# Layer 3 of a four-layer convolution/sequence kernel: transfers moved to the front of each time step, the logarithm moved ahead of the next exponentials, and the matmuls that open a sum put in separate places

## The chip, the cores and the metric

The kernel runs on one core of a Trainium2 chip. Five engines work from queues of their own, each strictly in the order written: TensorE (PE, with its weight loads shown as PEld), VectorE (DVE), ScalarE (ACT), GpSimd (POOL) and SyncE (SP), which in this part of the kernel only issues DMAs. An instruction that must wait holds everything behind it in its own queue. The metric is the device time of one execution in microseconds (us).

## The reference, cut to what matters

Four layers run one after another over `x` of shape (2, 128, 64, 64). Only the last one, layer 3, is touched. Each pixel's 128 channels are read as a sequence of 8 tokens of 16 channels, and a small state-space model runs along the tokens:

```
xi, z = split(seq @ in_proj_w.T)
xs    = silu(causal_conv(xi))                       # 32 channels
dt, Bm, Cm = split(xs @ x_proj_w.T, [1, 17])
dt    = softplus(dt @ dt_proj_w.T + dt_proj_b)
dA    = exp(dt[..., None] * A)                      # 32 channels x 16 states
dBx   = dt[..., None] * Bm[:, :, None, :] * xs[..., None]
h     = dA_t * h + dBx_t                            # token after token
y     = sum over states of h * C_t
out   = ((y + xs * D) * silu(z)) @ out_proj_w.T
```

The result goes through a group norm and a SiLU and is added to the layer's input.

## The kernel before, in words

Layer 3 works on 16 chunks (2 images x 8 chunks of 512 pixels). A chunk keeps its 512 pixels along the free dimension. Its 8 tokens are taken in 4 time steps, k = 0 to 3, of two neighbouring tokens each (o = 0 and 1; at k = 0 the first token needs no recursion). State is held as tiles of 128 partitions (4 states of a group x 32 channels) by 4 groups by 512 pixels, and the work on a tile is cut into two halves of 128x1024.

The order of the work is written out by hand: one loop over steps `s`, and in every step four places g = 0 to 3 (plus a tail, place 4). A place is named (k, g) here. At each place the loop issues fixed work, then what two tables hold: `first` (issued early in the place) and `extra` (issued at its end). `manual_schedule` keeps that order on every engine; waits come only from data and from buffers.

The fixed work of a step, for its own chunk:

- `mul` (POOL, L1278): A x h of the token before, 128x1024. `add` (L1283): D = D + that product, most on DVE, one half a step on POOL. `advance()` hands these out: it issues products until it has issued one DVE addition.
- `db_` (DVE, L1265): D of the **next** step times `dt x` taken from the PSUM tile `rx`; `rx_` (PE, L1261) spreads `dt x` of one token over the partitions. `rx` has two buffers.
- `da_` (ACT, L1271): four exponentials A = exp(dt x A) of the **next** step, read from `dtr`.
- `pc_` (PE, L1295, tile `q`) and `hc_` (DVE, L1300): product of A h with C, for the step **before**; `y_` (PE, L1313) adds it up in PSUM tile `y`, which has one buffer. The sums for the third unit and after come later, `y_(k, 3)` two steps on.

In `first` and `extra` stands the work that prepares later chunks, and what ends a chunk. `fut2` is the chunk two ahead, `fut` the next:

- `xs_`, `sz_` (PE into `misc`, SiLU on ACT) of `fut2`, in step 2. PSUM tile `misc` has one buffer, so each waits for the eviction before it.
- `dt_` (PE, then Abs and Relu on ACT), `e_exp` (ACT, L1211), `e_ln` (ACT, L1214): softplus. `dt_add` (POOL, L1217) finishes dt, `dtx_` (POOL, L1220) makes `e` = dt x xs, and `put` (SP, L1224) writes dt to a DRAM tile `ddt`.
- `b_` (PE L1184, copy on ACT L1191, then the DMA `rows<-bs` on SP, L1193), `c_`/`cb_`: B and B x C.
- `cbx_` (PE, into `misc`) and `ecb_` (DVE, L1251): the part of y that needs no recursion. `ecb_` overwrites `dt`, so it also waits until `put` has read it. `cbx_(1)` needs `misc` back from `ecb_(0)`.
- `load` (SP, L1244): `D<-rows`, 4 DMAs of 256 KB for one token of the step two ahead; six `D` buffers. `spread` (SP, L1232): `dtr<-ddt`, 8 DMAs of 64 KB (4 at k = 0) for the step two ahead; two buffers.
- `y0_` (PE, L1305): opens the sum y with D x xs and with `ecb_`'s result; `yg_` (DVE, L1318) gates y when it is done; `xr_`, `bn_` end the chunk.

On SP every DMA is bound to one of eight completion counters in turn, so one that is issued waits for the landing of the eighth before it.

Of the kernel before, what the change touches and what calls it, by code (L numbers as in the profile page):

```python
# [57 lines left out]
def conv_seq_kernel(ctx: ExitStack, tc: tile.TileContext, a: dict, out: bass.AP):  # L58
    nc = tc.nc
    mm = nc.tensor.matmul  # L60
# [4 lines left out]
    def gt(shape, name, pool=None, **kw):  # L65
        return (pool or gp).tile(shape, F32, tag=name, name=name, **kw)
# [14 lines left out]
    ident = cst[:, _CI : _CI + 128]  # L81
# [17 lines left out]
    with ExitStack() as c0:  # L99
# [36 lines left out]
        diag_d = gt([P, 2, P], "diag_d", wp)  # L136
# [347 lines left out]
        nk = len(chunks)  # L484
# [12 lines left out]
        with tc.manual_schedule():  # L497
            c, c1 = chunks[:2]
# [113 lines left out]
            for k, c in enumerate(chunks):  # L612
# [3 lines left out]
                def at(u):  # L616
                    return (c, u) if 0 <= u < 16 else ((old, u + 16) if u < 0 else (new, u - 16))
# [115 lines left out]
    with ExitStack() as c1:  # L733
# [272 lines left out]
        for n, j in enumerate(jobs):  # L1006
# [10 lines left out]
            if jobs[n - 1].layer == 1:  # L1017
                for ci in range(NCH):
                    c = Conv(jobs[n - 1].b, ci)
# [70 lines left out]
    with ExitStack() as c3:  # L1090
# [50 lines left out]
        diag_d = gt([P, P], "diag_d3", wp)  # L1141
# [10 lines left out]
        class Chunk3:  # L1152
# [148 lines left out]

            def y0_(self, i):
                self.y = ps.tile([P, T], F32, tag="y", name="y")
                for w, rhs in ((diag_d, self.xs), (ident, self.dt)):
                    mm(self.y, lhsT=w, rhs=rhs[:, i, :], start=w is diag_d, stop=False,  # L1305
                       skip_group_check=True)

            def y_(self, k, u):
                i, j = PLACE[k]
# [93 lines left out]
        with tc.manual_schedule():  # L1403
            c, c1 = chunks[:2]
            for i in range(2):
                c.xs_(i)
            for i in range(2):
                c.sz_(i)
            c.b_()
            for i in range(2):  # L1410
                c.dt_(i)
            c.e_exp()
            c.e_ln()
            c.dt_add()
            c.put()
            c.dtx_()
            c.spread(0)
            c.load(0, 0)
            c.load(0, 1)
            c.c_()  # L1420
            c.cb_()
            for i in range(2):
                c.cbx_(i)
                c.ecb_(i)
            for i in range(2):
                c1.xs_(i)
            c1.sz_(0)
            norms = [Norm(b) for b in range(B)]
            c.rx_(0, 0)
            for s in range(-1, len(steps) + 3):  # L1430
                (pc_, pk), (cc, ck), (nc_, nk) = at(s - 1), at(s), at(s + 1)
                (n2, n2k) = at(s + 2)
                ci, k = divmod(s, 4)
                fut = chunks[ci + 1] if s >= 0 and ci + 1 < len(chunks) else None
                fut2 = chunks[ci + 2] if ci + 2 < len(chunks) else None
                old = chunks[ci - 1] if ci > 0 else None
                nrm = norms[0] if ci in (NCH, NCH + 1) else None


                if cc is None:  # L1440
                    todo = []
                elif ck == 0:
                    todo = [("m", 1, 0), ("m", 1, 1), ("v", 1, 0), ("g", 1, 1)]
                elif ck == 3:
                    todo = [("m", 0, 0), ("m", 0, 1), ("v", 0, 0), ("g", 0, 1), ("m", 1, 0), ("m", 1, 1)]
                else:
                    todo = [("m", 0, 0), ("m", 0, 1), ("v", 0, 0), ("v", 0, 1), ("m", 1, 0),
                            ("m", 1, 1), ("v", 1, 0), ("g", 1, 1)]

                def advance():  # L1450

                    while todo:
                        w, o, hf = todo.pop(0)
                        if w == "m":
                            cc.mul(ck, o, hf)
                        else:
                            cc.add(ck, o, hf, V if w == "v" else G)
                        if w == "v":
                            return

                first, extra = {}, {}

                def more(key, *what, at=extra):
                    at.setdefault(key, []).extend(what)

                if cc is not None:
                    more((1, 2), lambda: cc.y0_(0), at=first)
                    more((3, 2), lambda: cc.y0_(1), at=first)  # L1470
                    more((3, 0), lambda: cc.yg_(0))
                if old is not None:
                    more((1, 0), lambda: old.yg_(1))
                    more((1, 2), old.xr_)
                    more((2, 0), old.bn_)
                if fut2 is not None and s >= 0:
                    more((2, 1), lambda: fut2.xs_(0))
                    more((2, 2), lambda: fut2.xs_(1))
                    more((2, 3), lambda: fut2.sz_(0))
                if fut2 is not None:  # L1480
                    more((3, 0), lambda: fut2.sz_(1), at=first)
                    more((3, 1), fut2.b_)
                    more((3, 2), lambda: fut2.dt_(0))
                    more((3, 3), lambda: fut2.dt_(1), fut2.e_exp)
                if fut is not None:
                    more((0, 0), fut.e_ln)
                    more((0, 1), fut.c_)
                    more((0, 2), fut.cb_, fut.dt_add, fut.dtx_)
                    more((0, 3), fut.put)
                    more((0, 3), lambda: fut.cbx_(0))  # L1490
                    more((1, 0), lambda: fut.ecb_(0), lambda: fut.cbx_(1))
                    more((1, 1), lambda: fut.ecb_(1))
                if 0 <= ci < B:
                    more((1, 3), lambda: nc.sync.dma_start(kept[ci], x[:, ci, :]))
                if n2 is not None:
                    more((k, 1), lambda: n2.load(n2k, 0))
                    more((k, 2), lambda: n2.load(n2k, 1))
                    more((k, 3), lambda: n2.spread(n2k))
                    more((k, 2), lambda: n2.rx_(n2k, 0), at=first)
                if nc_ is not None:  # L1500
                    more((k, 0), lambda: nc_.rx_(nk, 1), at=first)
                if ci == NCH:
                    more((2, 2), nrm.first)
                    more((2, 3), nrm.second)
                    more((2, 4), nrm.third)
                    more((3, 1), nrm.fourth)
                if ci == NCH + 1:
                    more((2, 3), *[lambda j=j: nrm.silu(j) for j in range(4)])
                    more((0, 0), lambda: nrm.load(0), lambda: nrm.load(1))
                    more((2, 4), lambda: nrm.store(0, G), lambda: nrm.load(2))  # L1510
                    more((3, 2), lambda: nrm.store(1, V), lambda: nrm.load(3))
                    more((3, 4), lambda: nrm.store(2, G), lambda: nrm.store(3, V))

                (older, ok) = at(s - 2)
                units = 0 if pc_ is None else 2 if pk == 0 else 4

                sums = {}
                for u in range(units):
                    g = (2 + u) if pk == 0 else max(2, u + 1) if pk == 2 else u + 1
                    sums.setdefault(g, []).append(u)  # L1520
                for g in range(4):
                    if g < units:
                        prepare()
                    if g == 0 and older is not None and ok:
                        older.y_(ok, 3)
                    for f_ in first.get((k, g), []):
                        f_()
                    for u in sums.get(g, []):
                        pc_.y_(pk, u)
                    if g < units:  # L1530
                        pc_.hc_(pk, g)
                    if nc_ is not None and nk != 3:
                        nc_.db_(nk, g // 2, g % 2)
                    elif nc_ is not None and g % 2 == 0:
                        nc_.db_(nk, 0, g // 2)
                    if g == 0 and nc_ is not None:
                        nc_.da_(nk)
                    if g < 3:
                        advance()
                    for f_ in extra.get((k, g), []):  # L1540
                        f_()
                while todo:
                    advance()
                for f_ in extra.get((k, 4), []):
                    f_()
                if s < 0:
                    prepare()
            n1 = norms[1]
            n1.load_all()
            n1.first()  # L1550
            n1.second()
            n1.third()
            n1.fourth()
            for j in range(4):
                n1.silu(j)
                n1.store(j, V)
# [111 lines left out]
```

## Time and profile before

| | us |
|---|---|
| median of the runs shown (3 runs, 6790.3 to 6802.03) | 6790.45 |
| the profiled execution | 6801.13 |
| its span, first to last instruction | 6799.3 |
| layer 3 in it, from about | 5629 to the end |
| busy in 5700 to 6660: PE / DVE / POOL / ACT, of 960 us | 793.8 / 755.7 / 695.9 / 408.0 |
| mean granted TensorE clock there | 0.86 |

The busy rows are read within the stage, since the four layers have different limits. A granted clock of 0.86 is a mean of full and half speed. Layer 3 is very regular: the instruction `dt_add` of the 15 chunks that are prepared inside the loop starts at 5703.17 for the first and 6663.00 for the last, so one chunk takes (6663.00 - 5703.17) / 14 = 68.56 us. Lines that begin with a time are instructions, with start, duration, engine, line, tiles; a bracket at the end is the engine's idle time before it and what ended that.

### The profile page before, as it was taken

The numbers are of one execution on the slowest core, as the hardware profiler recorded it, in microseconds if no ns is written. First come the engines' busy times: TensorE is split into PE (matmuls) and PEld (weight loads), VectorE is DVE, ScalarE is ACT, GpSimd is POOL, SyncE is SP. The second block draws the span as 40 slices with busy tenths as digits, with TensorE's granted clock in tenths as the row PEclk, the third lists the DMA queues.
The fourth block names the chain that finished last, engine by engine and source line by source line (L and its number), as shares of the span: only waits on it lengthen the run. The fifth ranks groups of instructions, "written<-read, shape, count | busy, mean of one in ns | idle before, by whom it ended". The sixth has DMA issues, their size and how long they took to land. (4 is left out here: it accounts for less than half of the span.)

```text
span 6799.3 us, 66250 instructions
## 1 busy us (share of the span) xinstructions
PE 5964.9 (88%) x19980; PEld 2797.7 (41%) x19980; DVE 5548.7 (82%) x4456; ACT 4472.3 (66%) x7737; POOL 5378.7 (79%) x2471
## 2 busy tenths in 40 slices
PE   8888888888888888888889999999999996888887
PEld 2222222222222222222248877887788881222221
DVE  7999999999999999999977665665566764877877
ACT  7887788877788777887765654554555553444442
POOL 6999999999999999999966665555566664777776
PEclk8888777877887778877789999999999996888987
DMA  6556655655666566665610000000000005665664
GB/s 183 144 148 162 164 148 143 150 145 144 157 152 153 145 150 154 155 149 144 155 47 1 5 3 1 1 1 1 1 1 1 1 1 128 150 157 137 171 148 124
DMA packets 397882, 700.60 MB, mean 103 GB/s; under 512 B 73801, under 2 KB 76242, under 8 KB 396882
## 3 DMA queue, kind: packets, MB, share of 16 engines
q1 hardware_dynamic: 396640, 694.32, 41.4%
q8 instruction: 157, 2.57, 0.2%
q14 instruction: 203, 1.66, 0.1%
q10 hardware_dynamic: 882, 2.04, 0.1%
HBM read 584.80 MB, written 111.28 MB: 102 GB/s over the span
## 5 line engine op out<-in xcount | busy, mean ns | idle before, releaser
L384 POOL TENSOR_TENSOR dbu<-dus,bs 128x1024 f32<-128x1024 f32 x1024 | 2447.1, 2439 | 117.4 <-DVE h L428 103.6
L428 DVE TENSOR_TENSOR_SCAN h<-da,hst,dbu 128x1024 f32<-128x1024 f32 x896 | 2092.6, 2342 | 86.8 <-ACT dbu L412 80.2
L397 ACT ACTIVATE da<-dts,aneg 128x512 f32<-128x512 f32 (+1 forms) x2048 | 1410.1, 689 | 356.3 <-DVE h L428 319.3
L924 POOL TENSOR_TENSOR sum<-sum,sc 128x1024 f32<-128x1024 f32 x384 | 906.7, 2361 | 491.7 <-ACT sc L919 487.9
L886 ACT COPY sc<-s 128x512 f32<-128x512 f32 x1024 | 597.6, 585 | 859.5 <-PE s L881 745.8
L881 PE MATMUL s<-q,k 128*128 128x256 f32 x4096 | 1052.0, 380 | 7.1 <-DVE k L858 3.5
L893 DVE TENSOR_TENSOR mx<-mx,s 128x512 f32<-128x512 f32 x896 | 610.0, 681 | 546.0 <-ACT sc L886 544.8
L451 PE MATMUL y<-hc,cst 128*32 128x512 f32 x4096 | 884.2, 758 | 193.2 <-DVE hc L440 180.1
L936 PE MATMUL av<-sc,v 128*128 128x256 f32 x4096 | 1049.5, 379 | 2.5 <-ACT sc L919 2.5
L440 DVE TENSOR_TENSOR hc<-h,pc 128x1024 f32<-128x1024 f32 x704 | 843.6, 1198 | 10.1 <-PE y L451 8.3
L881 PEld LDWEIGHTS s<-q,k 128*128 128x128 f32 x4096 | 776.6, 190 | 141.0 <-issue 29.0
L936 PEld LDWEIGHTS av<-sc,v 128*128 128x128 f32 x4096 | 768.8, 190 | 103.2 <-ACT sc L919 3.9
L438 POOL TENSOR_TENSOR hc<-h,cs 128x1024 f32<-128x1024 f32 x320 | 770.6, 2408 | 1.2 <-issue 1.2
L417 PE MATMUL pc<-xd,sel 16*128 16x512 f32 x1024 | 709.0, 783 | 1.5 <-DVE hc L440 1.3
L1278 POOL TENSOR_TENSOR A<-A,D 128x1024 f32<-128x1024 f32 x224 | 523.9, 2358 | 129.9 <-DVE D L1283 101.1
L916 DVE TENSOR_TENSOR sc<-sc,pm 128x1024 f32<-128x1024 f32 x512 | 620.9, 1214 | 0.9 <-PE pm L912 0.9
L919 ACT ACTIVATE sc<-sc 128x1024 f32<-128x1024 f32 x512 | 541.9, 1059 | 8.7 <-DVE sc L916 8.1
L341 PE MATMUL misc<-xd,w_dt 9*128 9x512 f32 x504 | 365.7, 812 | 127.8 <-ACT x L480 69.1
L451 PEld LDWEIGHTS y<-hc,cst 128*32 128x32 f32 x4096 | 126.3, 120 | 847.5 <-DVE hc L440 416.6
L1283 DVE TENSOR_TENSOR D<-D,A 128x1024 f32<-128x1024 f32 x128 | 282.6, 2208 | 130.9 <-POOL A L1278 130.9
L412 ACT ACTIVATE dbu<-hst,dbu,df 128x1 f32<-128x1 f32 x896 | 337.6, 377 | 62.4 <-POOL dbu L384 39.9
L1295 PE MATMUL q<-xs,lc 32*128 32x512 f32 x896 | 301.8, 687 | 36.0 <-DVE A L1300 35.9
(263 smaller groups left out, 7722.0 us busy)
## 6 DMA issues: line engine op xcount, KB each, us to landing
dts<-ddt SPq DMA_DIRECT2D x512, 256.0 KB, 5.4
dus<-ddu SPq DMA_DIRECT2D x512, 256.0 KB, 5.1
D<-rows SPq DMA_DIRECT2D x448, 256.0 KB, 5.9
bs<-rows SPq DMA_DIRECT2D x1024, 64.0 KB, 4.9
cs<-rows SPq DMA_DIRECT2D x1024, 64.0 KB, 3.3
ddt<-dt SPq DMA_DIRECT2D x128, 256.0 KB, 2.0
ddu<-dtu SPq DMA_DIRECT2D x128, 256.0 KB, 4.1
dtr<-ddt SPq DMA_DIRECT2D x448, 64.0 KB, 4.7
```

Of the source, the lines that this page charges most:

```text
L384: nc.gpsimd.tensor_mul(t, self.dus[q], _bc(self.bs[g], 1, [P, 2, T]))
L397: act(t[:, i, sl], self.dts[q][:, i, sl], AF.Exp, scale=an[:, g, 2 * q + i : 2 * q + i + 1])
L417: mm(t, lhsT=sel[32:48, 4 * g : 4 * g + 4, :].rearrange("p n d -> p (n d)"), rhs=self.xd[32:48, :], start=True, stop=True)
L428: nc.vector.tensor_tensor_scan(ho, ai, bi, init, ALU.mult, ALU.add)
L438: nc.gpsimd.tensor_mul(t, self.h[u], _bc(self.cs[gq(u)[0]], 1, [P, 2, T]))
L440: nc.vector.tensor_mul(t, self.h[u], _bc(self.pc[u // 2], 1, [P, 2, T]))
L451: mm(self.y[q // 2][r : r + 32, :], lhsT=sum4, rhs=self.hc[u][:, i, :], start=False, stop=(u % 8 >= 6), skip_group_check=True)
L881: mm(p[:, o, :], lhsT=j.k[m // 8][:, m % 8 * P : m % 8 * P + P], rhs=self.q, start=True, stop=True)
L893: nc.vector.tensor_max(self.mx, self.s[0][:, 0:2, :] if u == 1 else self.mx, self.p[u])
L916: nc.vector.tensor_sub(s, s, _bc(self.pm[:, :], 1, [P, 4, NQ]))
L924: nc.gpsimd.tensor_add(self.sum, self.s[0] if w == 1 else self.sum, self.s[w])
L936: mm(self.av, lhsT=self.job.v[m // 8][:, m % 8, :], rhs=self.s[u // 2][:, m % 4, :], start=(m == 0), stop=(m == 31))
```

## The change

Nothing is computed otherwise; instructions move to other places of the loop.

- SP: `spread`, then `load(.., 0)` of the step two ahead go to place 0, `load(.., 1)` to place 1 (before: `load` at 1 and 2, `spread` at 3).
- ACT: `e_ln` goes from (0, 0) of the next step to right behind `e_exp`, at (3, 2). `dt_` goes from (3, 2) and (3, 3) to (3, 1) and (3, 2); `b_` from (3, 1) to (3, 3), so behind the logarithm.
- POOL: `dt_add` and `dtx_` from (0, 2) to (0, 0), ahead of the POOL addition of step 0. `c_` and `cb_` go to (0, 0) and (0, 1).
- PE: both `rx_` of the step two ahead stand together at the end of place 3 (before: one at place 2, the other at place 0 of the following step). `xs_` and `sz_` go to places 0 to 3 of step 2. `y0_` is split: `y0_(0)` at (1, 1) and `y1_(0)` at (1, 3), both for i = 1 at (3, 1) (before: both at (1, 2) and both at (3, 2)).
- DVE: in place 3 `hc_` comes behind `db_`.
- Ahead of the loop: `sz_` of chunk 1 and both `rx_` of the first step.

```diff
             def y0_(self, i):
                 self.y = ps.tile([P, T], F32, tag="y", name="y")
-                for w, rhs in ((diag_d, self.xs), (ident, self.dt)):
-                    mm(self.y, lhsT=w, rhs=rhs[:, i, :], start=w is diag_d, stop=False,
-                       skip_group_check=True)
+                mm(self.y, lhsT=diag_d, rhs=self.xs[:, i, :], start=True, stop=False,
+                   skip_group_check=True)
+
+            def y1_(self, i):
+                mm(self.y, lhsT=ident, rhs=self.dt[:, i, :], start=False, stop=False,
+                   skip_group_check=True)
...
-            c1.sz_(0)
+            for i in range(2):
+                c1.sz_(i)
             norms = [Norm(b) for b in range(B)]
-            c.rx_(0, 0)
+            for o in range(2):
+                c.rx_(0, o)
...
                 if cc is not None:
-                    more((1, 2), lambda: cc.y0_(0), at=first)
-                    more((3, 2), lambda: cc.y0_(1), at=first)
+                    more((1, 1), lambda: cc.y0_(0), at=first)
+                    more((1, 3), lambda: cc.y1_(0), at=first)
+                    more((3, 1), lambda: cc.y0_(1), lambda: cc.y1_(1), at=first)
...
                 if fut2 is not None and s >= 0:
-                    more((2, 1), lambda: fut2.xs_(0))
-                    more((2, 2), lambda: fut2.xs_(1))
-                    more((2, 3), lambda: fut2.sz_(0))
+                    more((2, 0), lambda: fut2.xs_(0))
+                    more((2, 1), lambda: fut2.xs_(1))
+                    more((2, 2), lambda: fut2.sz_(0))
+                    more((2, 3), lambda: fut2.sz_(1))
                 if fut2 is not None:
-                    more((3, 0), lambda: fut2.sz_(1), at=first)
-                    more((3, 1), fut2.b_)
-                    more((3, 2), lambda: fut2.dt_(0))
-                    more((3, 3), lambda: fut2.dt_(1), fut2.e_exp)
+                    more((3, 1), lambda: fut2.dt_(0))
+                    more((3, 2), lambda: fut2.dt_(1), fut2.e_exp, fut2.e_ln)
+                    more((3, 3), fut2.b_)
                 if fut is not None:
-                    more((0, 0), fut.e_ln)
-                    more((0, 1), fut.c_)
-                    more((0, 2), fut.cb_, fut.dt_add, fut.dtx_)
+                    more((0, 0), fut.c_, fut.dt_add, fut.dtx_)
+                    more((0, 1), fut.cb_)
+                    more((0, 2), lambda: fut.cbx_(0))
                     more((0, 3), fut.put)
-                    more((0, 3), lambda: fut.cbx_(0))
                     more((1, 0), lambda: fut.ecb_(0), lambda: fut.cbx_(1))
                     more((1, 1), lambda: fut.ecb_(1))
...
                 if n2 is not None:
-                    more((k, 1), lambda: n2.load(n2k, 0))
-                    more((k, 2), lambda: n2.load(n2k, 1))
-                    more((k, 3), lambda: n2.spread(n2k))
-                    more((k, 2), lambda: n2.rx_(n2k, 0), at=first)
-                if nc_ is not None:
-                    more((k, 0), lambda: nc_.rx_(nk, 1), at=first)
+                    more((k, 0), lambda: n2.spread(n2k), lambda: n2.load(n2k, 0))
+                    more((k, 1), lambda: n2.load(n2k, 1))
+                    more((k, 3), lambda: n2.rx_(n2k, 0), lambda: n2.rx_(n2k, 1))
...
-                    if g < units:
+                    if g < min(units, 3):
                         pc_.hc_(pk, g)
...
+                    if g == 3 and units == 4:
+                        pc_.hc_(pk, g)
```

## The prediction

> **What bounds the kernel now.** I read the page's 40 slices first: layer 3 holds the last sixth of the span, and no engine there is full. Then the waits by engine, in 5760 to 6660 (engine and line, what it waited for: us in total, times, longest):
>
> ```profile
> POOL dt L1217 <- ACT e L1214: 146.8, 13, 12.6
> ...
> DVE D L1283 <- POOL A L1278: 109.1, 38, 7.5
> ...
> PE misc L1165 <- DVE dt L1251: 120.9, 13, 10.9
> ...
> ACT L1271 <- DMA dtr<-ddt: 115.7, 13, 10.3
> ```
>
> Once a chunk POOL stands about 11 us at `dt_add`, PE about 9 us at `cbx_(1)`, ACT 9 us at `da_`. The timeline of one chunk shows that it is one stall, handed on. ACT, POOL, SP, DVE, PE:
>
> ```profile
> 6512.19 1.06 ACT L1211 ACTIVATE e<-e 128x1024 f32<-128x1024 f32 x1
> 6518.37 4.27 ACT L1271 ACTIVATE A<-dtr,aneg 128x1024 f32<-128x1024 f32 x4 [5.13 <-DMA dtr<-ddt]
> ...
> 6523.95 1.06 ACT L1214 ACTIVATE e<-e 128x1024 f32<-128x1024 f32 x1
> ```
>
> ```profile
> 6501.23 9.32 POOL L1278 TENSOR_TENSOR A<-A,D 128x1024 f32<-128x1024 f32 x4
> 6510.62 2.36 POOL L1283 TENSOR_TENSOR D<-D,A 128x1024 f32<-128x1024 f32 x1
> 6525.09 2.34 POOL L1217 TENSOR_TENSOR dt<-dt,e 128x1024 f32<-128x1024 f32 x1 [12.10 <-ACT e L1214]
> 6527.50 2.34 POOL L1220 TENSOR_TENSOR e<-dt,xs 128x1024 f32<-128x1024 f32 x1
> 6529.80 4.64 POOL L1278 TENSOR_TENSOR A<-A,D 128x1024 f32<-128x1024 f32 x2
> ```
>
> ```profile
> 6502.62 0.34 SPq L1193 DMA_DIRECT2D rows<-bs  x1
> 6503.07 3.85 SPq L1244 DMA_DIRECT2D D<-rows  x8
> 6507.36 8.78 SPq L1232 DMA_DIRECT2D dtr<-ddt  x8
> 6516.25 3.68 SPq L1244 DMA_DIRECT2D D<-rows  x8
> 6527.45 0.34 SPq L1224 DMA_DIRECT2D ddt<-dt  x1
> ```
>
> ```profile
> 6532.18 3.35 DVE L1283 TENSOR_TENSOR D<-D,A 128x1024 f32<-128x1024 f32 x1 [7.53 <-POOL A L1278]
> ...
> 6536.04 0.67 DVE L1251 TENSOR_TENSOR dt<-e,misc 128x512 f32<-128x512 f32 x1
> ```
>
> ```profile
> 6525.26 1.12 PE L1261 MATMUL rx<-e,cst 32*128 32x512 f32 x2
> 6536.77 2.07 PE L1165 MATMUL misc<-cb,nsum 128*128 128x512 f32 x2 [10.39 <-DVE dt L1251]
> ...
> 6546.49 3.24 PE L1313 MATMUL y<-A,cst 128*32 128x512 f32 x4
> 6549.66 1.98 PE L1323 MATMUL misc<-sz,lo 128*128 128x512 f32 x4
> ```
>
> Read it in this order. SP's loads wait behind `rows<-bs`, so `dtr` of step 1 lands late and `da_` starts at 6518.37, 5.13 us late. The logarithm stands behind `da_` on ACT and ends at 6525.0. `dt_add` needs it, and POOL's products of step 1 stand behind `dt_add`: POOL is idle 12.10 us. DVE's addition waits 7.53 us for the product; `ecb_(0)` stands behind that addition; PE waits 10.39 us for `ecb_(0)`. After that gap PE runs at half speed: two-row groups take 2.07 us where the same groups took 1.12, until 6549.66, so for 12.8 us.
>
> **The clock I use.** t = 0 is POOL's first product of step 3, at 6493.30; the next chunk's is at 6562.65, t = 69.35. Before: `dt_add` starts at t = 31.8, `da_(1)` ends at 29.3, the product of step 1 starts at 36.5, DVE's addition ends at 42.2, `ecb_(0)` starts at 42.7.
>
> **The change part by part, for one chunk.**
>
> *Logarithm and `dt_`.* `yg_` before `y0_(1)` ends at 6499.63 (t = 6.3) and frees `y`. From there PE issues `y0_`, `y1_`, `dt_(0)`, one `pc_`, two `y_`, `dt_(1)`: seven groups of 1.05 us (the pitch in the rows at full clock), to t = 13.7. ACT then takes Abs and Relu (0.69 + 0.68), exp 1.06, table load 1.28, logarithm 1.06: t = 18.4 instead of 31.7. The number of table loads stays four a chunk (SiLU, exp, ln, exp), so that costs nothing. POOL is free at t = 17.25, so its wait falls from 12.1 to about 1 us.
>
> *POOL.* `dt_add` and `dtx_` 2.34 each, then the POOL addition that is now behind them 2.36, then the product: t = 25.4 to 27.8, against 36.5 to 38.9. `da_(1)` follows `b_`'s copy (0.57) and a table load (1.28): it runs t = 20.2 to 24.5, hence in time; its `dtr` is issued in step 3 ahead of `rows`. DVE gets to the addition when its own work of step 0 ends, at 6524.6 (t = 31.3) as now; it ends at about t = 33.
>
> *SP: the new wait.* `rows<-bs` now waits for a copy that stands behind the logarithm: t = 18.9 instead of 9.3. Behind it on SP stand 8 `dtr`, 8 `D`, and then `put`. Before, `put` was alone. What does that cost? In the timeline rows + 8 D + 8 dtr, 2816 KB, took from 6502.62 to the landing at 6518.1, 15.5 us. Rows + dtr + D + `put` are 3328 KB; at the same pace 18.3 us, so `put` lands at t = 37.2. The lower bound is 16 issues (4.01 + 3.68 us) and `put`'s median landing of 2.8: t = 30. I take 37.2, since DMAs of one burst share the engines. `ecb_(0)` must wait for it: start 37.2 instead of 42.7. The gain of 11 us on POOL is cut to 5.5 here.
>
> *PE and its clock.* From `y0_(1)` to its `cbx_(1)` PE took 6501.97 to 6526.38, 24.4 us, and gets `b_` in addition (1.05): it is free at t = 31.8 and waits 6.1 us for `ecb_(0)` at 37.9. Gaps in this layer of 2.17 us and less were followed by full-speed groups, those of 3.35 and more by half speed. So the clock still falls. I take the same 12.8 us at half speed.
>
> *`rx_` moved back.* In step 1 the `rx` of step 3 stood behind `cbx_`, `pc_`, `y0_`, `y1_`; it now stands behind `xr_` and two unpaired `y_` too. At half speed that is 12.8 us for `cbx_`, `pc_`, `y0_`, `y_` (3.24) and `xr_`, then at full speed `y1_` 1.0, `y_` 1.9, `rx` 1.05: ready at 37.9 + 16.8 = 54.7, used by `db_` to 55.8; the addition of step 2 behind it ends at 57.0, against 58.3 now. So 1.3 us of the gain are left here. Then it grows again: `bn_`, `hc_`, addition (0.69 + 1.13 + 1.2) end at 60.0, where they now end at 63.7, since `bn_` and `q` are no longer late; product 2.37 and POOL addition 3.22 end the step at 65.6. With the shortest half-speed stretch seen (5780.9 to 5788.3, 7.4 us) the same sum gives 62.8, against 66.4 for that chunk before.
>
> *The rest.* `xs_`/`sz_` one place earlier, `hc_` behind `db_` in place 3, `c_`/`cb_` earlier: no new work. `xs_(1)` waits for ACT behind `da_` as now (0.36 us), up to 2 us, covered by `q` having two buffers; the `c_` group ends at about t = 21, DVE reaches `cb_` at 20.4, under 1 us. Both are in DVE's margin before its addition; if PE were late by more, each would move the chunk one for one. The two groups ahead of the loop cost at most 2 us once.
>
> **Sum.** 69.4 - 65.6 and 66.4 - 62.8: 3.7 us a chunk, call it 4.0, since a gap of 6.1 instead of 10.4 should leave the shorter stretches more often. Fifteen chunks have the stall: 60 us. The profiled execution's 6801.13 becomes 6741; it lies 10.7 above the median of the runs, so the prediction is 6730.
>
> The Trainium skill says in "TensorE: Matmul & The Clock Gate", What's actually happening, that full clock comes back after about 3.4 us of sustained work. The row differs: 12.8 us of uninterrupted half-speed groups. By the rule the lag would be 1.7 us rather than 6.4, and by an estimate from that page the time would be some 40 us lower; no number here uses it.
>
> **Rivals.**
>
> *A. The clock never falls* (0.24). If `put` lands by t = 34.4, `ecb_(0)` ends by 35.1 and the gap is below 3.35 us. For it: 2.8 us median landing. Against: 2 MB are in flight ahead. Then `ecb_(0)` ends at 34.1, `rx` is ready at 45, the POOL/DVE chain runs through: 57.5 us a chunk, 11 less than the mean of 68.56, 165 us: 6625.
>
> *B. Slower: the clock falls at the other gap* (0.18). `y0_(1)` at (3, 1) waits for `yg_`. Where the rows stand now PE would idle 1.0 us there, but if PE comes out of step 2 early, up to 3.3. From 3.35 on the clock falls there, and everything up to `b_` runs at half speed: 3.7 to 6.4 us later (half of 7.4 and 12.8). `rows`, `put` and `ecb_(0)` come as much later, and 65.6 becomes 69.3 to 72. At the middle, 70.7, that is 1.35 us a chunk over now, 20 us: 6811. It decides from a delay of about 4 us on.
>
> The clock gate page of the Trainium skill, HAM oscillation, names idle gaps over about 3.4 us as what brings the clock down; the 3.35 us gap in the trace agrees, and that is the rule that speaks against this change.
>
> *C. Nothing gained* (0.08). `put` lands 4 us later than I take it (41 us), because `dtr`'s small packets slow the burst; then chunk time stays within 1 us: 6775 to 6800.
>
> **Numbers.** The forecast has 0.50, within 6690 to 6765 by its own bounds (2 to 6.7 us a chunk). A and the forecast are faster, 0.74; C and the edge of B are within 0.2% (about 14 us, what a measurement of this kernel can tell from no change), 0.08; the rest of B is slower, 0.18. The range 6628 to 6808 leaves out the lower part of A and the upper of B.
>
> **What would show it.** Right: POOL's idle at `dt_add` at 0 to 3 us, the logarithm directly behind the exponential, `ecb_(0)` waiting for `ddt<-dt`, PE's gap at `cbx_(1)` of 4 to 8 us with 2.08 us groups behind it, `db_` of step 3 waiting for `rx`. Wrong: a PE gap over 3.35 us ahead of `y0_` (B), a granted clock near 1.0 throughout (A), or ACT waiting for `dtr` in a new place.

## The result and the profile after

The changed kernel takes 6770.94 us (median; 6755.09 to 6785.65), the kernel before 6795.49 us beside it (6787.81 to 6802.03). The ratio is 0.9964, interval 0.9954 to 0.9975: 24.5 us faster, where the prediction had 60. The direction is right; the size is not.

Where the time went is best counted in the two profiled executions, from the first `dt_add` of layer 3, which stands ahead of the loop, to the end of the span, because layers 0 to 2 are the same. Before it is 1143.6 us, after 1114.2 us: 29.4 us. The distances between successive `dt_add` split it:

| stretch | before | after | gain |
|---|---|---|---|
| first `dt_add` to the first inside the loop | 47.4 | 31.8 | 15.6 |
| 11 regular chunks, without a normalisation in them | mean 67.94 | mean 65.55 | 26.3 |
| 3 chunks beside the group norm and the SiLU of the first image | 212.5 | 221.7 | -9.2 |
| last `dt_add` to the end | 136.3 | 139.6 | -3.3 |

The waits by engine of the changed kernel, in 5760 to 6640 (engine and line, what it waited for: us in total, times, longest):

```profile
POOL A L1278 <- DVE D L1283: 176.5, 55, 10.3
...
DVE D L1265 <- PE q L1295: 98.1, 25, 6.4
...
PE misc L1165 <- DVE dt L1251: 63.3, 13, 7.6
...
DVE dt L1251 <- DMA ddt<-dt: 37.0, 12, 5.8
PE y L1304 <- DVE sz L1321: 30.8, 12, 7.4
POOL dt L1217 <- ACT e L1214: 29.2, 13, 4.4
PE misc L1165 <- ACT xs L1172: 28.6, 13, 2.2
```

POOL's wait for the logarithm fell from 146.8 to 29.2 us and PE's for `ecb_(0)` from 120.9 to 63.3. In their place stand new rows: POOL's products wait for DVE's additions (176.5 us, where the same row had 82.4 in 5760 to 6660 before), DVE waits for `put` to land, PE waits for a SiLU at `xs_(1)` and for `yg_` at `y0_(1)`, and DVE's `db_` waits for PE. (Line numbers after L1304 are 3 higher than before.) One chunk in the timeline, ACT, POOL, SP, DVE, PE; t = 0, POOL's first product of step 3, is at 6123.30:

```profile
6139.25 1.06 ACT L1211 ACTIVATE e<-e 128x1024 f32<-128x1024 f32 x1
...
6141.62 1.06 ACT L1214 ACTIVATE e<-e 128x1024 f32<-128x1024 f32 x1
```

```profile
6142.76 2.36 POOL L1217 TENSOR_TENSOR dt<-dt,e 128x1024 f32<-128x1024 f32 x1 [2.20 <-ACT e L1214]
...
6150.71 4.70 POOL L1278 TENSOR_TENSOR A<-A,D 128x1024 f32<-128x1024 f32 x2
```

```profile
6143.18 0.34 SPq L1193 DMA_DIRECT2D rows<-bs  x1
6143.56 3.68 SPq L1232 DMA_DIRECT2D dtr<-ddt  x8
6147.35 3.68 SPq L1244 DMA_DIRECT2D D<-rows  x8
6151.36 0.34 SPq L1224 DMA_DIRECT2D ddt<-dt  x1
```

```profile
6157.28 0.68 DVE L1321 TENSOR_TENSOR sz<-sz,y 128x512 f32<-128x512 f32 x1
6160.66 0.69 DVE L1251 TENSOR_TENSOR dt<-e,misc 128x512 f32<-128x512 f32 x1 [2.70 <-DMA ddt<-dt]
...
6176.49 1.22 DVE L1265 TENSOR_TENSOR D<-D,rx 128x1024 f32<-128x1024 f32 x1 [5.96 <-PE q L1295]
```

```profile
6161.41 2.07 PE L1165 MATMUL misc<-cb,nsum 128*128 128x512 f32 x2 [4.81 <-DVE dt L1251]
...
6170.73 1.98 PE L1326 MATMUL misc<-sz,lo 128*128 128x512 f32 x4
...
6175.34 0.69 PE L1261 MATMUL rx<-e,cst 32*128 32x512 f32 x1
...
6181.76 1.12 PE L1165 MATMUL misc<-x,lm 128*128 128x512 f32 x2 [2.20 <-ACT xs L1172]
...
6194.48 2.08 PE L1304 MATMUL y<-xs,diag_d 128*128 128x512 f32 x2 [2.28 <-DVE sz L1321]
```

The trace names `q` as what released `db_`; `db_` reads `rx`, whose group ends beside it, so the wait is for `rx`. The chain of the prediction is there link by link: logarithm directly behind the exponential, `put` behind 16 transfers, `ecb_(0)` waiting for it, PE at half speed behind the gap, `rx` late for `db_`. The last two PE rows are not in the prediction: two waits of 2.2 us, the second with two half-speed groups behind it. The next chunk's t = 0 is at 6188.08, so this chunk takes 64.8 us, and nearly every regular one does: 64.8 to 65.3 in eight of eleven.

### The profile page after: what moved, and what is told of

Read it like the earlier page. It is cut to its first block, busy times and chain, and to the rows that moved or that the text cites. A ratio compares the mean times of both kernels' runs of the same rounds, so it can differ in the third digit from the quotient of the medians.

```text
span 6766.5 us, 66235 instructions
## 1 busy us (share of the span) xinstructions
PE 5937.2 (88%) x19980; PEld 2785.3 (41%) x19980; DVE 5486.3 (81%) x4456; ACT 4471.8 (66%) x7736; POOL 5390.1 (80%) x2471
## 5 line engine op out<-in xcount | busy, mean ns | idle before, releaser
L1265 DVE TENSOR_TENSOR D<-D,rx 128x1024 f32<-128x1024 f32 x224 | 269.0, 1212 | 173.0 <-PE q L1295 109.9
L1271 ACT ACTIVATE A<-dtr,aneg 128x1024 f32<-128x1024 f32 (+1 forms) x256 | 245.8, 1031 | 201.5 <-PE y L1316 103.8
```

## The experiments

Two theories stood against each other. One: the put's landing and the clock that falls behind it hold the chunk, as in the prediction. The other: the parts that the prediction priced at nothing (places of `xs_`/`sz_`, `y0_`, `rx_`, `dt_add`) take the time, because PE, DVE and POOL keep the written order. All ratios are to the kernel before on the same chip. "Layer 3" is first `dt_add` to end, "chunk" the median distance between `dt_add`s over seven regular chunks, both of the profiled execution. In e13, e14 and e17 the chunks alternate between about 60.5 and 62.4 us, and the median shows the shorter.

| kernel | ratio | interval | layer 3 | chunk |
|---|---|---|---|---|
| before | 1 | | 1143.6 | 67.0 |
| the change | 0.9964 | 0.9954 to 0.9975 | 1114.2 | 64.9 |
| e1 logarithm alone | 0.9871 | 0.9856 to 0.9885 | 1050.6 | 60.9 |
| e5 logarithm + `xs_`/`sz_` | 0.9948 | 0.9933 to 0.9963 | 1115.5 | 68.3 |
| e6 logarithm + `y0_` | 0.9915 | 0.9899 to 0.9932 | 1087.4 | 63.7 |
| e8 logarithm + earlier `put` | 0.9860 | 0.9845 to 0.9874 | 1035.1 | 61.2 |
| e7 logarithm + transfers | 0.9805 | 0.9791 to 0.9820 | 1008.9 | 58.2 |
| e16 e7 + `rx_` together | 0.9854 | 0.9839 to 0.9869 | 1042.9 | 61.5 |
| e17 e7 + `dt_add`, `dtx_` early | 0.9878 | 0.9861 to 0.9895 | 1057.4 | 60.5 |
| e2 change, `put` first | 0.9949 | 0.9934 to 0.9964 | 1099.9 | 66.5 |
| e3 change, SiLUs first | 0.9962 | 0.9948 to 0.9977 | 1117.8 | 67.0 |
| e4 change, `rx_` back | 0.9970 | 0.9961 to 0.9980 | 1117.7 | 64.9 |
| e12 change, PE kept busy | 0.9949 | 0.9934 to 0.9963 | 1094.2 | 64.8 |
| e9 change, `xs_`/`sz_` back | 0.9937 | 0.9922 to 0.9952 | 1093.2 | 65.0 |
| e10 e9 and `y0_`, `dt_`, `b_` back | 0.9927 | 0.9910 to 0.9943 | 1086.4 | 64.8 |
| e11 e9 and `rx_` back | 0.9912 | 0.9897 to 0.9927 | 1083.3 | 62.9 |
| e13 e10 and `rx_` back | 0.9870 | 0.9855 to 0.9884 | 1054.2 | 60.5 |
| e14 e13 and `hc_` back | 0.9873 | 0.9857 to 0.9890 | 1051.4 | 60.5 |
| e15 e13 and `c_` to `cbx_(0)` back | 0.9809 | 0.9795 to 0.9824 | 1006.0 | 58.2 |
| e18 e11 and `c_` to `cbx_(0)` back | 0.9905 | 0.9889 to 0.9922 | 1080.0 | 63.4 |

### e1: the logarithm's place alone

```diff
+more((3, 3), lambda: fut2.dt_(1), fut2.e_exp, fut2.e_ln)
-more((0, 0), fut.e_ln)
```

> The kernel before with one part of the change: the logarithm stands directly behind its exponential, in step 3; SP, PE, DVE and POOL keep their order. Theory 1 (the order on SP is what eats the gain: in the changed kernel the write of dt stands behind 16 loads, so ecb_ waits, PE idles over 3.35 us and falls to half speed): here the write of dt still goes out alone, so ecb_ does not wait for it, PE's gap at cbx_(1) falls from about 10 us to under 2, the clock stays, and a regular chunk falls from 67.5 us to about 60: 6795 becomes 6690 to 6710. Theory 2 (the new order of PE and DVE work, or the late dtr ahead of da_, sets the chunk; the logarithm alone frees little): POOL's wait moves from dt_add to the product behind it, which waits for da_; at most 2 to 3 us a chunk, 6755 to 6775.

One line moved in the kernel before is worth 1.3%, more than three times what the whole change brings. So the rest of the change loses on balance, and no theory of what bounds the changed kernel can stop at the logarithm.

### e2, e3, e4, e12: single repairs of the changed kernel

e2 puts `put` between `spread` and the loads; e3 lets the group norm's four SiLU passes go ahead of `sz_(1)` on ACT; e4 gives `rx_` its old places; e12 repeats `pc_`'s products of the latest unit twice ahead of `cbx_(1)` (the same values again, into the same tile), so that PE has work while it waits.

```diff
 # e2
-more((0, 3), fut.put)
+more((0, 0), fut.put)          # behind spread, ahead of load(.., 0)
 # e3
-more((2, 3), lambda: fut2.sz_(1))
+more((2, 3), lambda: fut2.sz_(1)) if ci != NCH + 1 else None
-more((2, 3), *[lambda j=j: nrm.silu(j) for j in range(4)])
+more((2, 3), *[lambda j=j: nrm.silu(j) for j in range(4)], lambda: fut2.sz_(1))
 # e4
-more((k, 3), lambda: n2.rx_(n2k, 0), lambda: n2.rx_(n2k, 1))
+more((k, 2), lambda: n2.rx_(n2k, 0), at=first)
+more((k, 0), lambda: nc_.rx_(nk, 1), at=first)
 # e12
-more((1, 0), lambda: fut.ecb_(0), lambda: fut.cbx_(1))
+more((1, 0), lambda: fut.ecb_(0), *[again] * 2, lambda: fut.cbx_(1))
```

> The changed kernel with the write of dt (put) issued between spread and the first load of step 0, so ahead of the 8 D loads. Theory 1: dt lands about 9 us earlier, ecb_(0) no longer waits for it (now 2.7 to 3.1 us), PE's gap of 4.8 us falls below 2.3, the clock does not fall, DVE's wait of 5.9 us for rx goes; a regular chunk falls from 64.9 to about 60: 6771 becomes 6700 to 6715. Theory 2: the wait is handed on to the D loads of step 2 or to the late rx; the chunk stays at 63 or more: 6745 to 6771.

> The changed kernel with one chunk altered: in the chunk where the first image is normalised, the four SiLU passes over x stand ahead of sz_(1) on ACT again, as they did in the kernel before. Theory N1 (the 85.5 us of that chunk come from POOL's first output addition, which waits 9.0 us for those SiLU passes, 2.9 before): 6 to 10 us come off this one chunk, and with it SP's wait for that addition, 27.6 us, shortens: 6771 becomes 6760. Theory N2 (that chunk is long because PE ran it at half speed): no change, 6766 to 6776.

> The changed kernel with rx_ back in its two old places (one token at place 2, the other at place 0 of the following step). Theory 1 (rx of step 3 stands behind xr_ and two y_ in PE's half-speed stretch): DVE's wait of 5.9 us ahead of db_ of step 3 goes, 2 to 4 us a chunk: 6771 becomes 6725 to 6745. Theory 2 (PE is late with everything in that stretch, so that q or y is waited for in its place): within 10 us of 6771.

> The changed kernel with the product of the last prepared q tile made twice more on PE ahead of cbx_(1): about 4 us of matmuls that change no value, in PE's gap of 4.8 us. Theory G (the gap is what brings the clock down, as the prediction had it): the groups behind it run at full speed, DVE's wait of 5.9 us for PE goes, 2 to 4 us a chunk: ratio 0.988 to 0.992. Theory H (the clock falls by what PE has done in the stretch before, and gaps of 1.1 us are followed by half speed too): the groups behind stay at half speed, 0.996 to 1.000.

The intervals of all four overlap that of the change. In e2 DVE no longer waits for the put, but thirteen of its `db_` now wait for the loads behind it (38.6 us in 5760 to 6600), PE's gap at `cbx_(1)` stays at 3.5 to 5.3 us in the regular chunks with half speed behind it, and the two waits of 2.2 us on PE stay. e3 shortens the three chunks of the group norm to 215.0 us; whether ACT's order there costs the 9.2 us is left open by it. Its regular chunks, which its edit does not touch, take 67.0 us in the median against 64.9, so the chunk column of one execution can be 2 us off by itself. e4 alone gains nothing that can be told; PE still stands 2.2 us at `xs_(1)` there. e12 shortens the gap and does not save the clock (PE):

```profile
6095.06 3.70 PE L1411 MATMUL q<-xs,lc 32*128 32x512 f32 x8
6099.80 2.08 PE L1165 MATMUL misc<-cb,nsum 128*128 128x512 f32 x2 [1.04 <-DVE dt L1251]
6101.80 2.08 PE L1295 MATMUL q<-xs,lc 32*128 32x512 f32 x4
6103.81 2.08 PE L1304 MATMUL y<-xs,diag_d 128*128 128x512 f32 x2
```

The gap at `cbx_(1)` is 1.04 us instead of 5, the groups behind it still take 2.08 us, and the chunk stays at 64.8. So a gap of several us is not needed for half speed to follow, and DVE's wait for the put does not hold the chunk by itself: taking either away moves almost nothing. What the chunk would take with PE at full speed there, neither run shows, since the half-speed groups are in both.

### e5 to e8: one part of the change added to the logarithm

```diff
 # e5, against e1
-more((2, 1), lambda: fut2.xs_(0))
-more((2, 2), lambda: fut2.xs_(1))
-more((2, 3), lambda: fut2.sz_(0))
-more((3, 0), lambda: fut2.sz_(1), at=first)
+more((2, 0), lambda: fut2.xs_(0))
+more((2, 1), lambda: fut2.xs_(1))
+more((2, 2), lambda: fut2.sz_(0))
+more((2, 3), lambda: fut2.sz_(1))
 # e6
-more((1, 2), lambda: cc.y0_(0), at=first)
-more((3, 2), lambda: cc.y0_(1), at=first)
+more((1, 1), lambda: cc.y0_(0), at=first)
+more((1, 3), lambda: cc.y1_(0), at=first)
+more((3, 1), lambda: cc.y0_(1), lambda: cc.y1_(1), at=first)
 # e7
-more((k, 1), lambda: n2.load(n2k, 0))
-more((k, 2), lambda: n2.load(n2k, 1))
-more((k, 3), lambda: n2.spread(n2k))
+more((k, 0), lambda: n2.spread(n2k), lambda: n2.load(n2k, 0))
+more((k, 1), lambda: n2.load(n2k, 1))
 # e8
-more((0, 3), fut.put)
+more((0, 2), fut.put)          # between the two loads of step 0
```

> The logarithm alone (6703 us) plus one more part of the change: xs_ and sz_ of the chunk two ahead one place earlier. Theory P (the part of the gain that the full change loses is lost on PE, which now waits inside its own order: 2.2 us at xs_(1) for the SiLU behind da_, 2.3 us ahead of y0_(1)): PE shows the 2.2 us wait at xs_(1) in every chunk; 15 x 2 to 3 us, 6703 becomes 6730 to 6750. Theory S (it is lost on SP: transfers first, rows and the write of dt late): within 10 us of 6703.

> The logarithm alone (6703 us) plus the split of y0_ and its new places. Theory P: PE stands about 1 to 2 us longer ahead of y0_(1), and the sum of step 2 comes later; 6703 becomes 6715 to 6735. Theory S: within 10 us of 6703.

> The logarithm alone (6703 us) plus the new places of spread and load on SP. b_ keeps its old place, so rows goes out early. Theory S: dt's write stands behind 16 loads of step 0 and ecb_ waits longer for it than the 1.2 to 1.7 us now; PE's gap grows above 4 us; 6703 becomes 6730 to 6760. Theory P: the loads only come earlier, ACT no longer waits for dtr (8 us a chunk), nothing waits longer: 6690 to 6710.

> The logarithm alone (6703 us), and the write of dt between the two loads of step 0 instead of behind them: no part of the change, but the wait that it still has. ecb_(0) waits 1.2 to 1.7 us for that write, and PE's gap of 3.5 to 3.8 us is followed by half speed. If the clock is worth what the prediction put on it (6 us a chunk at 12.8 us of half speed), the gap at about 2.2 us leaves it up: 57 us a chunk, 6703 becomes 6650 to 6670. If the half-speed stretch is covered by DVE's own work there: 6685 to 6705.

Against e1 the places of `xs_`/`sz_` cost 0.77%, those of `y0_` 0.44%, the earlier `put` nothing that can be told, and the transfers gain 0.66%. e5's row for `xs_(1)` in 5760 to 6600, and the same row of e7, where `xs_` stands at its old place:

```profile
PE misc L1165 <- ACT xs L1172: 27.1, 12, 2.8
```

```profile
POOL dt L1217 <- ACT e L1214: 42.5, 14, 6.1
...
PE misc L1165 <- DVE dt L1251: 18.0, 14, 3.4
...
PE misc L1165 <- ACT xs L1172: 4.3, 12, 0.4
...
DVE dt L1251 <- DMA ddt<-dt: 2.9, 1, 2.9
```

At the old place PE waits 0.36 us for the eviction of `misc`; one place earlier it waits 2.2, or 2.8 once, with all of its queue behind it. e7 beats both kernels: 58.2 us a chunk, the put waited for once, PE's gap at `cbx_(1)` 1.3 us in the mean (18.0 / 14). With `b_` at its old place, ahead of the logarithm, transfers first do not make anything wait for the put, although it lands 5.9 us after its issue in the median.

### e9 to e11: parts of the change taken back together

e9 takes back `xs_`/`sz_`; e10 also `y0_`, `dt_` and `b_`; e11 instead of these `rx_` (edits as above, reversed, and what stands ahead of the loop with them; `b_` goes back to (3, 1), `dt_` to (3, 2) and (3, 3)).

> The changed kernel with xs_ and sz_ back in their old places. Theory P (the places of xs_ cost what the logarithm alone lost when they were added, 0.8% of the time): PE's wait of 2.2 us at xs_(1) goes to 0.4, the ratio to the kernel before falls from 0.996 to 0.988 to 0.991. Theory Q (in the full change PE is held up by y0_ and rx_ anyway, so xs_ alone gives nothing back): 0.994 to 0.997.

> The changed kernel with xs_, sz_, y0_ and, since y0_ has to stand ahead of it, dt_ and b_ back in their old places; what is left of the change is the logarithm, the transfers, rx_ together, c_, cb_, dt_add, dtx_ earlier and the order of hc_ and db_. Theory P: close to the logarithm with the transfers (0.9805): 0.979 to 0.985. Theory Q (rx_ or the late rows are what costs): 0.988 to 0.994.

> The changed kernel with xs_, sz_ and rx_ back. rx_ back alone changed nothing measurable (0.9970 against 0.9964). Theory P: as with xs_ alone, 0.988 to 0.991. Theory R (rx_ shows its cost only when the PE wait at xs_(1) is gone): 0.983 to 0.987.

e9 is 0.9937, e4 (only `rx_` back) 0.9970, both together in e11 0.9912, with a chunk of 62.9 us. Each of the two largely covers the other: with `rx_` together the chunk stays at 64.8 to 65.0 in e9, e10 and e12, and with `xs_`/`sz_` early it is 64.9 in e4. But 0.9927 in e10 was still far from e7's 0.9805, and what is left between those two was open.

### e13 to e18: what is left between e7 and the change

```diff
 # e14, against e13
-if g < min(units, 3):
+if g < units:
     pc_.hc_(pk, g)
 # e15 against e13, e18 against e11
-more((0, 0), fut.c_, fut.dt_add, fut.dtx_)
-more((0, 1), fut.cb_)
-more((0, 2), lambda: fut.cbx_(0))
+more((0, 1), fut.c_)
+more((0, 2), fut.cb_, fut.dt_add, fut.dtx_)
 more((0, 3), fut.put)
+more((0, 3), lambda: fut.cbx_(0))
 # e16, against e7
-more((k, 2), lambda: n2.rx_(n2k, 0), at=first)
-more((k, 0), lambda: nc_.rx_(nk, 1), at=first)
+more((k, 3), lambda: n2.rx_(n2k, 0), lambda: n2.rx_(n2k, 1))
 # e17, against e7
-more((0, 2), fut.cb_, fut.dt_add, fut.dtx_)
+more((0, 0), fut.dt_add, fut.dtx_)
+more((0, 2), fut.cb_)
```

> The changed kernel with xs_/sz_, y0_/dt_/b_ and now rx_ at their old places. Against the log+transfers kernel (0.9805) three things are left: c_, dt_add, dtx_, cb_, cbx_(0) one place earlier, hc_ behind db_ in place 3, y0_'s order. Theory R (both rx_ at the end of place 3 are what keeps the chunk at 64.8 us in four of the variants): the period falls to 58 to 60 us, ratio 0.981 to 0.985. Theory C (dt_add ahead of the POOL addition stands 6.8 us a chunk for the logarithm, 94.9 us in 14 waits with xs_ and y0_ back): ratio 0.987 to 0.991, that wait stays over 5 us a chunk.

> As the one before, with hc_ ahead of db_ in place 3 again. Left of the change beside log and transfers: only c_, dt_add, dtx_, cb_, cbx_(0) one place earlier. If hc_'s order costs (PE's next product waits for q, which hc_ frees a db_ of 1.2 us later), 0.002 to 0.005 lower than the one before; if not, the same within 0.0015. Theory C says it is still 0.986 or more, theory R 0.981 to 0.983.

> As the first, with c_, cb_, dt_add, dtx_, cbx_(0) at their old places and hc_ behind db_ as changed. Left beside log and transfers: only hc_'s order. Theory C: back at 0.980 to 0.983, POOL's wait for the logarithm 42 us in all as in log+transfers, period 58.2. Theory R says the same as for the first run, so no change against it beyond 0.0015. If hc_'s order is what costs, 0.984 or more.

> The kernel before with the logarithm's place, the transfers' places and both rx_ at the end of place 3, nothing else. Theory R: about 64.8 us a chunk, ratio 0.988 to 0.991, db_ of the next step waits for rx, and the products behind it for q. If rx_ together costs only in company of the other moves: 0.980 to 0.983, period 58 to 59.

> The kernel before with the logarithm's and the transfers' places and dt_add, dtx_ alone ahead of the POOL addition at (0, 0); c_, cb_, cbx_(0) stay. If POOL's order is what cost 0.6% between the runs before (its wait at dt_add 5.14 us instead of 2.71, the addition of 2.36 us behind it): period about 60.5, ratio 0.986 to 0.988. If it was c_, cb_, cbx_(0) on PE and DVE: period 58.2, ratio 0.980 to 0.982.

> The changed kernel with xs_/sz_, rx_ and c_, dt_add, dtx_, cb_, cbx_(0) at their old places: beside logarithm and transfers only y0_ split and early, dt_ a place earlier, b_ behind the logarithm, hc_ behind db_. With xs_ and rx_ alone at their old places it was 0.9912. If y0_/dt_/b_ cost 0.4% on their own, as when added to the logarithm alone: 0.984 to 0.987, and PE waits ahead of y0_(1) or at cbx_(1) stay. If they cost only because dt_add stood early: 0.980 to 0.983. If dt_add early was right once dt_ is early: 0.990 or more.

e15 is back at 0.9809, so the ledger closes: with logarithm and transfers in place, `hc_`'s order costs nothing (e14 against e13), and three groups cost about half a per cent to one per cent each; `xs_`/`sz_`, the fourth, was added to the logarithm alone (e5, 0.77%). `c_`, `cb_` and `cbx_(0)` cost nothing that can be told: e17 without them is no faster than e13 and e14 with them. A few rows show each mechanism.

`dt_add` ahead of the POOL addition (e17, 0.73% over e7). POOL in e17, then in e15, where the addition comes first:

```profile
6132.05 2.37 POOL L1217 TENSOR_TENSOR dt<-dt,e 128x1024 f32<-128x1024 f32 x1 [5.15 <-ACT e L1214]
6134.50 2.37 POOL L1220 TENSOR_TENSOR e<-dt,xs 128x1024 f32<-128x1024 f32 x1
6136.82 2.38 POOL L1283 TENSOR_TENSOR D<-D,A 128x1024 f32<-128x1024 f32 x1
```

```profile
6150.51 2.36 POOL L1283 TENSOR_TENSOR D<-D,A 128x1024 f32<-128x1024 f32 x1
6155.59 2.38 POOL L1217 TENSOR_TENSOR dt<-dt,e 128x1024 f32<-128x1024 f32 x1 [2.72 <-ACT e L1214]
```

The addition was filler while POOL waits for the logarithm; put behind `dt_add`, it lengthens POOL's wait by 2.43 us, and the chunk goes from 58.2 to 60.5. That is theory C of e13's expectation. e18 against e11 says where it ends: beside the early `dt_` (with `y0_` and `b_` moved too) the early `dt_add` changes the time by 0.07%, inside both intervals. So in the full change, where `dt_` is early, `dt_add` is not what costs.

`y0_`, `dt_`, `b_` (e18, 0.96% over e15). SP and DVE in e18, then in e15:

```profile
6123.78 0.34 SPq L1193 DMA_DIRECT2D rows<-bs  x1
...
6131.80 0.40 SPq L1224 DMA_DIRECT2D ddt<-dt  x1
```

```profile
6140.89 0.69 DVE L1251 TENSOR_TENSOR dt<-e,misc 128x512 f32<-128x512 f32 x1 [2.66 <-DMA ddt<-dt]
```

```profile
6141.86 0.34 SPq L1193 DMA_DIRECT2D rows<-bs  x1
...
6157.99 0.34 SPq L1224 DMA_DIRECT2D ddt<-dt  x1
```

```profile
6166.65 0.67 DVE L1251 TENSOR_TENSOR dt<-e,misc 128x512 f32<-128x512 f32 x1
```

In e18 `b_` stands behind the logarithm: `rows` goes out 8.0 us ahead of the put, the 16 loads lie between, and `ecb_(0)` waits for the put, 14 times for 40.3 us in all. In e15 `rows` is out 16.1 us ahead, the loads between are all issued 3.5 us before the put, which lands after 5.6 us instead of 9.1, and here nothing waits for it (in 5760 to 6600 twice, for 3.0 us in all). PE's gap at `cbx_(1)` is 3.92 us against 1.12. The split of `y0_` is in e18 as well; e6 has it without `b_` and `dt_` at 0.44% over e1, so not all of the 0.96% is `b_`'s, and the shares within this group were not measured apart.

`rx_` together (e16, 0.49% over e7). DVE, then PE in e16:

```profile
6015.52 1.22 DVE L1265 TENSOR_TENSOR D<-D,rx 128x1024 f32<-128x1024 f32 x1 [4.95 <-PE q L1295]
```

```profile
6010.62 1.98 PE L1323 MATMUL misc<-sz,lo 128*128 128x512 f32 x4
6012.53 1.90 PE L1313 MATMUL y<-A,cst 128*32 128x512 f32 x4
6014.37 0.69 PE L1261 MATMUL rx<-e,cst 32*128 32x512 f32 x1
```

`rx` now stands behind `xr_` and two groups of y, and `db_` waits 4.95 us for it; the trace names `q` as releaser, but the `rx` groups end beside it, and `db_` reads `rx`. Such waits hold 89.0 us in 25 times in e16; in e7 `db_` waits for PE twice, for 1.4 us in all. The same row is the one of 98.1 us in the changed kernel.

## Why the prediction was right and wrong

**The stall and its cure: right.** The logarithm ended at t = 19.4 (forecast 18.4), POOL's wait at `dt_add` was 2.20 us (about 1), `ecb_(0)` started at t = 37.4 (37.2), held by `put`, PE's gap was 4.81 us (6.1) with 9.3 us at half speed behind it (12.8 taken), `rx` was there at t = 53.2 (54.7), and the chunk took 64.8 us (65.6 from 69.4). In e18, where `b_` stands behind the logarithm, the put is waited for 14 times, in e15, where it stands ahead, twice; `y0_` and `dt_` differ between the two as well, so that `b_` is the reason is read from SP's order and not shown apart.

**The sum's second term: wrong.** "66.4 - 62.8" did not come: the long and the short chunks of the kernel before (65.9 to 70.5 us, mean 67.94) both became 64.8 to 65.3 us, three of the eleven 66.4 to 67.8, and no regular chunk is below 64.8. The forecast's 65.6 for a long chunk is nearly the mean of the regular ones, 65.55; what failed is that the short ones would gain as much.

The step that failed is **"The rest"**, priced at no time with "`xs_(1)` waits for ACT behind `da_` as now (0.36 us), up to 2 us, covered by `q` having two buffers", together with the `rx_` step, which left `db_`'s wait inside the chunk as a fixed cost. PE does stand 2.20 us at `xs_(1)`, as bounded, but `q`'s buffers do not cover it: `sz_`, `y0_(1)`, `dt_` and both `rx_` stand behind it in PE's queue as well as the products for `q`. Added to the logarithm alone it costs 0.77%.

In the full change this cost hides beside the late `rx`: e9 and e4 take back one of the two and leave the chunk at 65.0 and 64.9, and e11 takes back both and gives 62.9 us and 0.9912, with layer 3 shorter than before by 1143.6 - 1083.3 = 60.3 us. That these two together hold the missing size is shown; that e11 lands on the forecast's very numbers (62.8, and 6730 / 6790.45 = 0.9911) is partly luck, since e11 is another kernel and its half-speed stretches are not the short ones that the 62.8 was worked out with (by the granted clock they last 13.7 us or more in its regular chunks).

**The multiplication: wrong.** 4.0 us, rounded up from 3.7, was applied to fifteen chunks alike. Eleven regular ones gave 2.4, the first gave 15.6, and the three beside the group norm, which the profile before shows at 67.0 to 72.8, lost 9.2 together. They have other limits and needed a price of their own. Two side sums are uneven too: B's 1.35 us is taken from one chunk of 69.35 while A's 11 us is taken from the mean of 68.56, and the "some 40 us" is not worked out, where 6.4 less 1.7 over fifteen chunks would be 70.

**What was not asked.** The late put does come with the logarithm's new place, as the prediction had it, and the half-speed stretch stays. e1 has both, with `b_` and the transfers at their old places: the put lands 9.0 us after its issue in the median. DVE's waits in 5760 to 6600, and PE, in e1:

```profile
DVE dt L1251 <- DMA ddt<-dt: 15.2, 10, 3.0
```

```profile
6067.30 2.07 PE L1165 MATMUL misc<-cb,nsum 128*128 128x512 f32 x2 [3.76 <-DVE dt L1251]
```

Yet e1 gains 1.3%, and 2.0% with the transfers (e7). So the stall that the prediction weighed most is not what separates the change from e1; the neighbouring moves are, and they were never priced on their own.

**The rivals.** A (the clock never falls): not seen; even in e7, with a gap of 1.11 us, PE falls to half speed at `cbx_(1)`. That its chunk of 58.2 us is nearly A's 57.5 is luck: it comes with the clock down, one wait for the put, and `rx` ready in time for `db_`. B (a fall of the clock ahead of `y0_(1)`): its place was right, 2.28 us and two groups at half speed in most chunks, but the stretch is short: `y0_` and `y1_` take 3.6 us from 6194.48, where two groups at the full-speed pitch of 1.05 would take 2.1, so its price is about 1.5 us (an estimate from these rows) and not 3.7. C (put lands at 41): no, 37.4.

The row behind B's point of decision failed as well: "2.17 us and less were followed by full-speed groups, those of 3.35 and more by half speed". In the changed kernel 2.20 us at `xs_(1)` is mostly followed by full speed and 2.28 us at `y0_(1)` by half speed, and in e5 the same 2.20 us is followed by half speed in 8 of 11 chunks. The Trainium skill, in "TensorE: Matmul & The Clock Gate", What's actually happening, says that the clock is set by how busy PE was, watched in a free-running window of 3413 ns. The runs agree in so far as equal gaps end differently, and as the granted clock in the traces changes only in steps of 3.41 us (last section); how busy a window must be, they do not show.

## What to carry to other kernels

Where engines keep the written order, price each moved instruction by what it waits for at its new place and by everything queued behind it; "no new work" is not "no cost", and work that stood ahead of a wait may have been its filler. A change of many moves is worth taking apart: here one moved line and three moved transfers are worth 2.0%, and the other moves, each defensible alone, hand 1.6% of it back. Their costs overlap, so undoing one at a time in the full change shows little (0.06 to 0.27%); adding one at a time to the logarithm, with or without the transfers, shows each (0.4 to 1.0%).

## What the runs showed of the hardware

- The granted clock fell behind gaps of about one microsecond. e7, PE:

```profile
6007.60 2.08 PE L1165 MATMUL misc<-cb,nsum 128*128 128x512 f32 x2 [1.11 <-DVE dt L1251]
6009.60 2.08 PE L1295 MATMUL q<-xs,lc 32*128 32x512 f32 x4
```

- Filling the wait with products on 32 partitions (e12) did not hold it either: 1.04 us of gap and half speed behind it.
- The granted clock in these traces is full or half and nothing between, and in layer 3 its half-speed stretches are whole multiples of 3.41 us: around `cbx_(1)` 13.7 to 23.9 us in most chunks of the kernel before, 10.2 us in most of the change and of e12, 6.8 us in most of e7; at `y0_(1)` of the change 3.4 us. The chunk that keeps coming back may have to do with this step: 19 steps are 64.85 us (the change, e4, e9, e10, e12), 18 are 61.4 (e16), 20 are 68.3 (e5, and the longest regular chunks of e3). If a chunk settles on whole steps, a small repair shows nothing until it is worth a step. No run tests this, and the chunks of e2, e6 and e11 fit no whole number.
- How long a DMA takes to land depends on what was issued just ahead of it: the put's median was 2.8 us before, 3.4 in e2, where it goes out behind eight `dtr` and ahead of the loads of `D`, and 9.1 in e18, where it goes out behind those loads as well (issued at 6131.80, waited for by DVE until 6140.89).
